# A fused attention block: the weighted sum moved between the two score passes, and the softmax denominator summed on GpSimd

## The chip, the core and the metric

The kernel runs on one core of one Trainium2 chip. The metric is device time in microseconds (us), the median of three runs. A profiled execution, recorded by the hardware profiler, has a time of its own.

The engines of the core are PE (TensorE, the matrix engine, with PEld for its weight loads), DVE (VectorE), ACT (ScalarE) and POOL (GpSimd); SP issues transfers. Each engine takes its instructions in the order in which the program has them, so an instruction that waits holds up everything behind it on that engine. Matmuls write to PSUM, a memory of eight banks per partition (a 128 x 512 float32 tile fills one).

## The reference

Layer norm with a modulation, causal attention with 32 query heads in 8 groups that share keys and values, a gated residual, then a second norm and a routed low-rank feed-forward part. The change is inside attention:

```python
q = _apply_rope((x @ Wq).reshape(b, t, 32, 32).transpose(0, 2, 1, 3), cos, sin)
k = _apply_rope((x @ Wk).reshape(b, t, 8, 32).transpose(0, 2, 1, 3), cos, sin)
v = (x @ Wv).reshape(b, t, 8, 32).transpose(0, 2, 1, 3)
...
scores = jnp.einsum('bhqd,bhkd->bhqk', q, k_h) / math.sqrt(HEAD_DIM)
scores = jnp.where(causal[None, None], jnp.finfo(scores.dtype).min, scores)
attn = jax.nn.softmax(scores, axis=-1)
ctx = jnp.einsum('bhqk,bhkd->bhqd', attn, v_h)
```

There are t = 2048 tokens, in float32; a head has 32 dimensions, and each of the 8 groups has 4 query heads, which together fill the 128 partitions.

## The kernel before

Three phases follow one another: norm and projections, attention, and the output projection with the feed-forward part. The attention phase lies between about 455 us and 2340 us of the profiled execution.

**Steps.** Attention is cut into 32 steps: for each group `g` of 8, four blocks `qb` = 0 to 3 of 512 queries. "Step 2" below is a step with `qb` = 2. A step looks at `nk = 4 * (qb + 1)` key tiles `kc` of 128 keys (4, 8, 12 and 16).

**Two score passes.** The softmax needs each query's maximum before it can exponentiate. The first pass (`maxima_units`, lines L344 to L378) computes scores with queries on the partitions: a unit is 4 matmuls (L358) for 128 queries and up to 512 keys, in two tiles `sm` of two banks each, which DVE reduces (L368; on the diagonal after adding the causal mask, L367). The second pass (`weights`, L407) computes them again with keys on the partitions: 4 matmuls (L414) into two tiles `sc`, to which small bfloat16 matmuls add the negated maxima (L422) and the causal mask (L431, on diagonal key tiles). ACT exponentiates each `sc` tile into `et` (L438).

**Sums.** `weighted_sum` (L444) multiplies `et` by the values into `po` (4 matmuls, L447). For odd `kc` POOL adds `et` of this key tile into `et` of the one before (L453), and `total` (L455) multiplies each such pair by a matrix of ones into `pd` (4 matmuls, L459): the denominators.

**Order.** While a step runs the second pass, it runs the first pass of the next step in between: step 0 has 8 units of the next step for its 4 key tiles, step 1 has 12 for 8, step 2 has 16 for 12, step 3 has 4 for 16. Per key tile the program has: units of the next step's maxima, `weights(kc)`, `weighted_sum(kc - 1)`, and on odd `kc` `total(kc - 3)` (`unit`, L464). At the end of a step `shift_rows` (L380) turns the next step's maxima into matmul rows: a cast, a subtraction, a cast, a subtraction and a cast on DVE (L384 to L388, on 128 x 16 elements), 4 transposes on PE (L391, tile `px`), and a copy `nt` (L395). `finish` (L472) then does the last sums, ACT copies `po` to `ctx` (L476), DVE takes the reciprocal `rd` of `pd` (L478) and POOL multiplies (L479). After each step 1, half of a modulation vector is computed (`mod_column_half` or `gate_half`, L121 to L146).

**Buffers.** `sm`, `sc`, `px` and the modulation tiles share one rotation of three two-bank PSUM tiles (`ps_s`, tag `sc`), so a tile is written only when the one three before it has been read. `po` and `pd` have a bank each. `et` has four buffers.

The scheduler of the language may move an instruction ahead of others on its engine; the order above is that of the program text.

Of the kernel before, what the change touches and what calls it, by code (L numbers as in the profile page):

```python
# [9 lines left out]
F32 = mybir.dt.float32  # L10
BF16 = mybir.dt.bfloat16
# [5 lines left out]
P = 128  # L17
# [3 lines left out]
HD = 32  # L21
# [3 lines left out]
QB = 512  # L25
# [9 lines left out]
def adaln_block_kernel(  # L35
# [16 lines left out]
    nc = tc.nc  # L52
# [68 lines left out]
    def mod_column_half(pool, pspool, tag, i, half):  # L121

        rows = mod_rows(pool, pspool, tag, i, half)
        pst = pspool.tile([P, 512], F32, tag=tag, name=f"modpt_{i}_{half}")
        for j in range(4):
            nc.tensor.matmul(
                pst[:, j : j + 1], rows[:, j * P : (j + 1) * P], ones_p[:, 0:1],
                start=True, stop=True,
            )
        dst = mod_cols[i][:, half * 4 : half * 4 + 4]  # L130
        if i in (1, 4):
            nc.vector.tensor_scalar_add(dst, pst[:, 0:4], 1.0)
        else:
            nc.vector.tensor_copy(dst, pst[:, 0:4])
# [34 lines left out]
    def modulate(dst, ps, scale, shift, k):  # L169
# [11 lines left out]
    q_t = [  # L181
        qpool.tile([P, T], F32, tag=f"q{g}", name=f"q{g}") for g in range(NG)
    ]

    with tc.tile_pool(name="kv", bufs=1) as kvpool:
# [4 lines left out]
        with tc.tile_pool(name="wqkv", bufs=1) as wp, tc.tile_pool(  # L190
            name="a_x", bufs=3
# [13 lines left out]
            with tc.tile_pool(name="m_w", bufs=4) as mp, tc.tile_pool(  # L205
                name="m_ps", bufs=2, space=PSUM
# [5 lines left out]
            with tc.tile_pool(name="a_h", bufs=2) as hp, tc.tile_pool(  # L212
                name="a_t", bufs=3
            ) as tp, tc.tile_pool(name="a_pt", bufs=2, space=PSUM) as ps_t, tc.tile_pool(
                name="a_pm", bufs=3, space=PSUM
# [76 lines left out]
        for i in (2, 5):  # L292
            gates[i] = gpool.tile([P, D], F32, tag=f"gate{i}", name=f"gate{i}")
        with tc.tile_pool(name="b_k", bufs=2) as kp, tc.tile_pool(
            name="b_e", bufs=4
        ) as ep, tc.tile_pool(name="b_s", bufs=2) as bp, tc.tile_pool(
            name="b_w", bufs=4
        ) as mp, tc.tile_pool(name="b_c", bufs=1) as bc, tc.tile_pool(
            name="b_ps", bufs=3, space=PSUM
# [80 lines left out]
            def shift_rows(n, g, qb, neg):  # L380

                nb = nbs[n % 2]
                rest = bp.tile([P, 4, 4], F32, tag="rest", name=f"rest_{g}_{qb}")
                nc.vector.tensor_copy(nb[:, :, :, 0], neg)  # L384
                nc.vector.tensor_sub(rest, neg, nb[:, :, :, 0])
                nc.vector.tensor_copy(nb[:, :, :, 1], rest)
                nc.vector.tensor_sub(rest, rest, nb[:, :, :, 1])
                nc.vector.tensor_copy(nb[:, :, :, 2], rest)  # L388
                px = ps_s.tile([P, 4, P], BF16, tag="sc", name=f"px_{g}_{qb}")
                for t in range(4):  # L390
                    nc.tensor.transpose(  # L391
                        px[:, t, :], nb[:, t].rearrange("p h r -> p (h r)"), ident_h
                    )
                nt = bp.tile([P, QB], BF16, tag="nt", name=f"nt_{g}_{qb}")
                nc.vector.tensor_copy(nt, px.rearrange("p t q -> p (t q)"))  # L395
                return nt

            def attend_units(g, qb, kr, nt):
                nk = 4 * (qb + 1)
                po = ps_o.tile([P, QB], F32, tag="po", name=f"po_{g}_{qb}")  # L400
                pd = ps_o.tile([P, QB], F32, tag="pd", name=f"pd_{g}_{qb}")
                ets = {}

                def offset(kc):
                    return max(0, kc * P - qb * QB)

                def weights(kc):  # L407

                    off = offset(kc)
                    ps = score_tiles(f"sc_{g}_{qb}_{kc}")  # L410
                    q0 = qb * QB
                    for j in range(4):
                        rows = slice(j * HD, (j + 1) * HD)
                        nc.tensor.matmul(  # L414
                            ps[j // 2][:, j % 2, off:],
                            kr[rows, kc * P : (kc + 1) * P],
                            q_t[g][rows, q0 + off : q0 + QB],
                            start=True, stop=False,
                        )
                    for j in range(4):  # L420
                        rows = slice(j * HD, (j + 1) * HD)
                        nc.tensor.matmul(  # L422
                            ps[j // 2][:, j % 2, off:], ones_h[rows, :], nt[rows, off:],
                            start=False, stop=(kc < 4 * qb),
                        )
                    if kc >= 4 * qb:
                        for c in range(4):
                            w = (c + 1) * HD
                            for j in range(4):
                                rows = slice(j * HD, (j + 1) * HD)  # L430
                                nc.tensor.matmul(  # L431
                                    ps[j // 2][:, j % 2, off : off + w],
                                    pick[rows, c, :], later[rows, c, :w],
                                    start=False, stop=(c == 3),
                                )
                    et = ep.tile([P, 4, QB], F32, tag="et", name=f"et_{g}_{qb}_{kc}")
                    for pr in range(2):
                        nc.scalar.activation(  # L438
                            et[:, 2 * pr : 2 * pr + 2, off:], ps[pr][:, :, off:],
                            AF.Exp, scale=1.0 / math.sqrt(HD),  # L440
                        )
                    ets[kc] = et

                def weighted_sum(kc):  # L444
                    off, et = offset(kc), ets[kc]
                    for j in range(4):
                        nc.tensor.matmul(  # L447
                            po[j * HD : (j + 1) * HD, off:], v_sb[:, kc, g, :], et[:, j, off:],
                            start=(kc == 0), stop=(kc == nk - 1),
                        )  # L450
                    if kc % 2 == 1:
                        a = ets[kc - 1]
                        nc.gpsimd.tensor_add(a[:, :, off:], a[:, :, off:], et[:, :, off:])  # L453

                def total(kc):  # L455

                    off, et = offset(kc), ets[kc]
                    for j in range(4):
                        nc.tensor.matmul(  # L459
                            pd[j * HD : (j + 1) * HD, off:], ones_k, et[:, j, off:],  # L460
                            start=(kc == 0), stop=(kc == nk - 2),
                        )

                def unit(kc):  # L464
                    if kc < nk:
                        weights(kc)
                    if 1 <= kc <= nk:
                        weighted_sum(kc - 1)
                    if kc >= 3 and kc % 2 == 1:
                        total(kc - 3)  # L470

                def finish():  # L472
                    unit(nk)
                    unit(nk + 1)
                    ctx_sb = bp.tile([P, QB], F32, tag="ctx", name=f"ctx_{g}_{qb}")
                    nc.scalar.copy(ctx_sb, po)  # L476
                    rd = bp.tile([P, QB], F32, tag="rd", name=f"rd_{g}_{qb}")
                    nc.vector.reciprocal(rd, pd)  # L478
                    nc.gpsimd.tensor_mul(  # L479
                        q_t[g][:, qb * QB : (qb + 1) * QB], ctx_sb, rd  # L480
                    )

                return [lambda kc=kc: unit(kc) for kc in range(nk)], finish


            rest = [(i, half) for i in (2, 3, 4, 5) for half in range(2)]
# [4 lines left out]
            for u in maxima_units(0, 0, 0, krs[0], state):  # L491
                u()
            nt = shift_rows(0, 0, 0, state["neg"])
            for n, (g, qb) in enumerate(steps):
                now, finish = attend_units(g, qb, krs[g], nt)
                ahead = []
                if n + 1 < len(steps):
                    g1, qb1 = steps[n + 1]
                    ahead = maxima_units(n + 1, g1, qb1, krs[g1], state)
                if qb == 1 and g + 1 < NG:  # L500
                    krs[g + 1] = keys(g + 1)
                done = 0
                for k, u in enumerate(now):
                    upto = len(ahead) * (k + 1) // len(now)
                    for a in ahead[done:upto]:
                        a()
                    done = upto
                    u()
                if n + 1 < len(steps):
                    nt = shift_rows(n + 1, g1, qb1, state["neg"])  # L510
                finish()
                if qb == 1:
                    i, half = rest[g]
                    if i in (3, 4):
                        mod_column_half(mp, ps_s, "sc", i, half)
                    else:
                        gate_half(mp, ps_s, "sc", i, half)


    with tc.tile_pool(name="c_w", bufs=1) as wp, tc.tile_pool(  # L520
# [146 lines left out]
```

## Time and profile before

| | us |
|---|---|
| runs | 2663.64, 2665.29, 2681.99 |
| median of the three | 2665.29 |
| the profiled execution | 2676.34 |
| its span, first to last instruction | 2674.6 |
| PE busy in the span | 2369.8 |
| DVE busy | 1267.6 |
| ACT busy | 631.5 |
| POOL busy | 634.8 |

One instance of each step, cut from one `ctx` copy (L476) to the next: step 2 from 1030.42 to 1112.23, step 3 to 1168.20, step 0 of the next group to 1207.97, step 1 to 1266.80.

How to read the profile: a group row gives line, engine, operation, tiles as output<-inputs, shapes and count, then busy time and the mean duration in ns of one, then idle time just before and what ended it. A timeline row gives start, duration, engine, line, operation, tiles, shapes and count of merged instructions, and in brackets the idle time before with its releaser. PEclk is the share of full speed granted to the TensorE clock. A float32 matmul appears as two matmul instructions, so 4 matmuls show as x8. Busy time of PE is modelled from starts, and pipelined matmuls overlap.

### The profile page before, as it was taken

To read this page: it belongs to the slowest core of one execution; us is meant where nothing else is said; L and a number is where in the kernel's file an instruction comes from. 1 tells how busy PE (TensorE), PEld (TensorE's weight loads), DVE (VectorE), ACT (ScalarE), POOL (GpSimd) and SP (SyncE) were. 2 spreads that over 40 slices of the span, in tenths; PEclk is the share of its full clock that TensorE was granted. 3 is DMA by queue.
4 is the path that set the end of the run, shared out by engine and by line. 5 is a ranking of instruction groups with operands and counts; after the bars stand their busy time and mean duration, and the time that the engine had idled before them with its cause. 6 is when DMAs were issued, how large, how long until landed. Compare 5 with 4: busy or idle time off the path is not lost.

```text
span 2674.6 us, 35449 instructions
## 1 busy us (share of the span) xinstructions
PE 2369.8 (89%) x15480; PEld 1081.7 (40%) x15480; DVE 1267.6 (47%) x2096; ACT 631.5 (24%) x869; POOL 634.8 (24%) x224
## 2 busy tenths in 40 slices
PE   6999997888888888888898888889888888889998
PEld 2888885323332333232333323223322322244544
DVE  3434324554554355446536544643654465243434
ACT  1001000224222422322241233224123322400101
POOL 0000001224323522432351243235123423500000
PEclk8999997789778978978896998889689788999999
DMA  7001002000000000000000000000000000021111
GB/s 277 27 24 36 12 5 63 0 33 1 16 32 1 17 1 32 1 17 5 28 14 4 32 1 17 9 24 11 7 32 1 1 1 1 23 105 47 48 63 48
DMA packets 29819, 74.73 MB, mean 28 GB/s; under 512 B 2784, under 2 KB 8032, under 8 KB 28640
## 3 DMA queue, kind: packets, MB, share of 16 engines
q1 hardware_dynamic: 25104, 65.03, 7.7%
q10 hardware_dynamic: 4560, 7.44, 0.8%
q8 instruction: 122, 2.00, 0.3%
q14 instruction: 33, 0.27, 0.0%
HBM read 55.68 MB, written 8.39 MB: 24 GB/s over the span
## 4 chain that ended last, share of the span: by engine, by line
PE 70%; DVE 21%; issue 4%; DMA 2%; ACT 2%; POOL 0%; SPq 0%; ACTq 0%; DVEq 0%; POOLq 0%
PE sc L414 14%; DVE mx L368 14%; PE po L447 11%; PE pq L271 10%; PE sm L358 10%; PE pw L546 8%; PE pd L459 5%; PE sc L422 3%; DVE rd L478 2%; PE pv L248 2%; ACT et L438 2%; PE sc L431 1%; PE pr L259 1%; DVE sm L367 1%; PE pa L570 1%
## 5 line engine op out<-in xcount | busy, mean ns | idle before, releaser
L368 DVE TENSOR_REDUCE mx<-sm 128x2 f32<-128x1024 f32 (+3 forms) x640 | 662.0, 1061 | 565.5 <-PE sm L358 558.6
L453 POOL TENSOR_TENSOR et<-et,et 128x2048 f32<-128x2048 f32 (+2 forms) x160 | 584.2, 3651 | 1088.4 <-ACT et L438 572.2
L438 ACT ACTIVATE et<-sc 128x1024 f32<-128x1024 f32 (+3 forms) x640 | 538.4, 893 | 1209.0 <-PE sc L431 614.5
L414 PE MATMUL sc<-q,kr 32*128 32x512 f32 (+3 forms) x2560 | 587.5, 648 | 137.8 <-DVE mx L368 129.4
L358 PE MATMUL sm<-kr,q 32*128 32x512 f32 (+3 forms) x2560 | 475.7, 665 | 73.3 <-DVE mx L368 66.7
L414 PEld LDWEIGHTS sc<-q,kr 32*128 32x128 f32 x2560 | 200.6, 205 | 489.1 <-DVE mx L368 208.2
L447 PE MATMUL po<-et,v_sb 128*32 128x512 f32 (+3 forms) x2560 | 368.5, 617 | 0.0
L358 PEld LDWEIGHTS sm<-kr,q 32*128 32x128 f32 x2560 | 177.6, 214 | 392.8 <-issue 159.5
L546 PE MATMUL pw<-wo,q 128*128 128x512 f32 x512 | 226.1, 599 | 12.1 <-DVE wo L533 12.1
L367 DVE TENSOR_TENSOR sm<-sm,causal 128x256 f32<-128x256 f32 x256 | 105.6, 424 | 272.1 <-PE sm L358 272.0
L271 PE MATMUL pq<-h_t,wq 128*128 128x256 f32 x1024 | 231.5, 379 | 0.0
L422 PE MATMUL sc<-nt,ones_h 32*128 32x512 bf16 (+3 forms) x1280 | 225.6, 390 | 0.0
L271 PEld LDWEIGHTS pq<-h_t,wq 128*128 128x128 f32 x1024 | 194.6, 190 | 26.5
L459 PE MATMUL pd<-et,ones_k 128*32 128x512 f32 (+1 forms) x1280 | 191.7, 677 | 1.1 <-POOL et L453 1.1
L546 PEld LDWEIGHTS pw<-wo,q 128*128 128x128 f32 x512 | 96.6, 192 | 129.8 <-issue 118.4
L478 DVE RECIPROCAL rd<-pd 128x512 f32<-128x512 f32 x32 | 107.4, 3358 | 62.3 <-PE pd L459 62.3
L275 DVE TENSOR_TENSOR u<-pq,cs 128x256 f32<-128x256 f32 x80 | 33.9, 424 | 215.2 <-PE pq L271 215.1
L447 PEld LDWEIGHTS po<-et,v_sb 128*32 128x32 f32 x2560 | 55.8, 115 | 142.7 <-issue 132.1
L431 PE MATMUL sc<-later,pick 32*128 32x64 bf16 (+3 forms) x2048 | 108.9, 212 | 0.0
L304 POOL MEMSET ones_h<- 128x128 bf16 x1 | 0.2, 204 | 433.1 <-DVE q L260 433.1
L550 DVE TENSOR_TENSOR cx<-pw,cx 128x512 f32<-128x512 f32 x32 | 22.1, 692 | 166.8 <-PE pw L546 162.7
L172 ACT ACTIVATE h_t<-pt,mod,mod 128x128 f32<-128x128 f32 x64 | 27.8, 457 | 260.1 <-PE pt L229 258.4
(101 smaller groups left out, 1273.4 us busy)
## 6 DMA issues: line engine op xcount, KB each, us to landing
wmod<-in_wmod_dram SPq DMA_DIRECT2D x48, 512.0 KB, 5.7
xt<-in_x_dram SPq DMA_DIRECT2D x16, 512.0 KB, 4.3
kr<-k SPq DMA_DIRECT2D x32, 256.0 KB, 4.4
cx<-in_x_dram SPq DMA_DIRECT2D x16, 512.0 KB, 4.4
out_dram<-ot SPq DMA_DIRECT2D x16, 512.0 KB, 2.9
wq<-in_wq_dram ACTq DMA_DIRECT2D x8, 512.0 KB, 9.8
wo<-in_wo_dram SPq DMA_DIRECT2D x8, 512.0 KB, 7.2
wv_sb<-in_wv_dram ACTq DMA_DIRECT2D x1, 1024.0 KB, 10.1
```

The lines of the kernel that those rows point to most:

```text
L271: nc.tensor.matmul(ps, w, h_t[:, k, :], start=(k == 0), stop=(k == NC - 1))
L358: nc.tensor.matmul(ps[j // 2][:, j % 2, :nk], q_t[g][rows, q0 : q0 + P], kr[rows, kc * QB : kc * QB + nk], start=True, stop=True,)
L368: nc.vector.tensor_reduce(mx[:, 2 * pr : 2 * pr + 2, kc], ps[pr][:, :, :nk], AX.X, ALU.max)
L414: nc.tensor.matmul(ps[j // 2][:, j % 2, off:], kr[rows, kc * P : (kc + 1) * P], q_t[g][rows, q0 + off : q0 + QB], start=True, stop=False,)
L422: nc.tensor.matmul(ps[j // 2][:, j % 2, off:], ones_h[rows, :], nt[rows, off:], start=False, stop=(kc < 4 * qb),)
L431: nc.tensor.matmul(ps[j // 2][:, j % 2, off : off + w], pick[rows, c, :], later[rows, c, :w], start=False, stop=(c == 3),)
L438: nc.scalar.activation(et[:, 2 * pr : 2 * pr + 2, off:], ps[pr][:, :, off:], AF.Exp, scale=1.0 / math.sqrt(HD),)
L447: nc.tensor.matmul(po[j * HD : (j + 1) * HD, off:], v_sb[:, kc, g, :], et[:, j, off:], start=(kc == 0), stop=(kc == nk - 1),)
L453: nc.gpsimd.tensor_add(a[:, :, off:], a[:, :, off:], et[:, :, off:])
L459: nc.tensor.matmul(pd[j * HD : (j + 1) * HD, off:], ones_k, et[:, j, off:], start=(kc == 0), stop=(kc == nk - 2),)
L478: nc.vector.reciprocal(rd, pd)
L546: nc.tensor.matmul(ps, q_t[k][:, t * P : (t + 1) * P], wo_sb[k][:, cols], start=(k == 0), stop=(k == NC - 1),)
```

## The change

The denominators are no longer summed by PE over pairs. Key tile 0 writes its exponentials into a tile of its own (`sum`, two buffers), POOL adds those of every other key tile into it, and one denominator matmul per head is made per step. `et` has three buffers in place of four. Per key tile, the weighted sum of the tile before now comes ahead of `weights(kc)`, after the maxima units. The denominator, the reciprocal and the multiplication (`divide`) are put off to key tile 2 of the next step, and the multiplication is on DVE. `px`, the denominator and the modulation tiles now share one bank (`ps_o`, tag `px`) in place of the rotation's tiles. The modulation halves move to key tile 3 of step 2.

```diff
-            name="b_e", bufs=4
+            name="b_e", bufs=3
...
-                px = ps_s.tile([P, 4, P], BF16, tag="sc", name=f"px_{g}_{qb}")
+                px = ps_o.tile([P, 4, P], BF16, tag="px", name=f"px_{g}_{qb}")
...
-                    et = ep.tile([P, 4, QB], F32, tag="et", name=f"et_{g}_{qb}_{kc}")
+                    if kc == 0:
+                        et = ep.tile([P, 4, QB], F32, tag="sum", name=f"sum_{g}_{qb}", bufs=2)
+                    else:
+                        et = ep.tile([P, 4, QB], F32, tag="et", name=f"et_{g}_{qb}_{kc}")
...
-                    if kc % 2 == 1:
-                        a = ets[kc - 1]
+                    if kc > 0:
+                        a = ets[0]
                         nc.gpsimd.tensor_add(a[:, :, off:], a[:, :, off:], et[:, :, off:])
 
-                def total(kc):
-
-                    off, et = offset(kc), ets[kc]
+                def last():
+
+                    weighted_sum(nk - 1)
+                    ctx_sb = bp.tile([P, QB], F32, tag="ctx", name=f"ctx_{g}_{qb}")
+                    nc.scalar.copy(ctx_sb, po)
+                    return ctx_sb
+
+                def divide(ctx_sb):
+
+                    pd = ps_o.tile([P, QB], F32, tag="px", name=f"pd_{g}_{qb}")
                     for j in range(4):
                         nc.tensor.matmul(
-                            pd[j * HD : (j + 1) * HD, off:], ones_k, et[:, j, off:],
-                            start=(kc == 0), stop=(kc == nk - 2),
+                            pd[j * HD : (j + 1) * HD, :], ones_k, ets[0][:, j, :],
+                            start=True, stop=True,
                         )
...
                     nc.vector.reciprocal(rd, pd)
-                    nc.gpsimd.tensor_mul(
-                        q_t[g][:, qb * QB : (qb + 1) * QB], ctx_sb, rd
-                    )
+                    nc.vector.tensor_mul(q_t[g][:, qb * QB : (qb + 1) * QB], ctx_sb, rd)
...
-                for k, u in enumerate(now):
-                    upto = len(ahead) * (k + 1) // len(now)
+                for kc in range(nk):
+                    upto = len(ahead) * (kc + 1) // nk
                     for a in ahead[done:upto]:
                         a()
                     done = upto
-                    u()
+                    if kc > 0:
+                        weighted_sum(kc - 1)
+                    weights(kc)
+                    if kc == 2 and behind is not None:
+                        behind()
+                        behind = None
+                    if kc == 3 and qb == 2:
+                        i, half = rest[g]
+                        if i in (3, 4):
+                            mod_column_half(mp, ps_o, "px", i, half)
+                        else:
+                            gate_half(mp, ps_o, "px", i, half)
                 if n + 1 < len(steps):
                     nt = shift_rows(n + 1, g1, qb1, state["neg"])
-                finish()
-                if qb == 1:
-                    i, half = rest[g]
-                    if i in (3, 4):
-                        mod_column_half(mp, ps_s, "sc", i, half)
-                    else:
-                        gate_half(mp, ps_s, "sc", i, half)
+                ctx_sb = last()
+                behind = lambda divide=divide, ctx_sb=ctx_sb: divide(ctx_sb)
+            behind()
```

In the instruction order that the scheduler makes of the changed program, the first of the four denominator matmuls of a step 3 stands earlier than in the text: behind the first two maxima units of the next step 0 and ahead of that step's first score matmul (in seven of the eight groups; the last step has no next one). In a step 3, for key tiles without a maxima unit, the first score matmul of `kc` stands ahead of `weighted_sum(kc - 1)` and the other three behind it. On DVE, one reduction or mask addition of key tile 3 stands between the reciprocal and the multiplication of `divide`, the others behind.

More of the change, by code (lines that the diff above doesn't have):

```diff
@@ L400, in attend_units @@
                 po = ps_o.tile([P, QB], F32, tag="po", name=f"po_{g}_{qb}")
-                pd = ps_o.tile([P, QB], F32, tag="pd", name=f"pd_{g}_{qb}")
                 ets = {}
@@ L450, in weighted_sum @@
                         )
-                    if kc % 2 == 1:
-                        a = ets[kc - 1]
+                    if kc > 0:
+                        a = ets[0]
                         nc.gpsimd.tensor_add(a[:, :, off:], a[:, :, off:], et[:, :, off:])
-                def total(kc):
-                    off, et = offset(kc), ets[kc]
+                def last():
[5 more added lines that the diff above has]
+                    pd = ps_o.tile([P, QB], F32, tag="px", name=f"pd_{g}_{qb}")
                     for j in range(4):
                         nc.tensor.matmul(
-                            pd[j * HD : (j + 1) * HD, off:], ones_k, et[:, j, off:],
-                            start=(kc == 0), stop=(kc == nk - 2),
-                        )
[L464 to L476, printed above, removed]
+                            pd[j * HD : (j + 1) * HD, :], ones_k, ets[0][:, j, :],
+                            start=True, stop=True,
+                        )
                     rd = bp.tile([P, QB], F32, tag="rd", name=f"rd_{g}_{qb}")
                     nc.vector.reciprocal(rd, pd)
-                    nc.gpsimd.tensor_mul(
-                        q_t[g][:, qb * QB : (qb + 1) * QB], ctx_sb, rd
-                    )
-                return [lambda kc=kc: unit(kc) for kc in range(nk)], finish
+                    nc.vector.tensor_mul(q_t[g][:, qb * QB : (qb + 1) * QB], ctx_sb, rd)
+                return nk, weights, weighted_sum, last, divide
             rest = [(i, half) for i in (2, 3, 4, 5) for half in range(2)]
@@ L493, in adaln_block_kernel @@
             nt = shift_rows(0, 0, 0, state["neg"])
+            behind = None
             for n, (g, qb) in enumerate(steps):
-                now, finish = attend_units(g, qb, krs[g], nt)
+                nk, weights, weighted_sum, last, divide = attend_units(g, qb, krs[g], nt)
                 ahead = []
@@ L507, in adaln_block_kernel @@
                     done = upto
-                    u()
+                    if kc > 0:
[3 more added lines that the diff above has]
+                        behind()
+                        behind = None
+                    if kc == 3 and qb == 2:
[4 more added lines that the diff above has]
+                            gate_half(mp, ps_o, "px", i, half)
                 if n + 1 < len(steps):
                     nt = shift_rows(n + 1, g1, qb1, state["neg"])
-                finish()
-                if qb == 1:
-                    i, half = rest[g]
-                    if i in (3, 4):
-                        mod_column_half(mp, ps_s, "sc", i, half)
-                    else:
-                        gate_half(mp, ps_s, "sc", i, half)
+                ctx_sb = last()
+                behind = lambda divide=divide, ctx_sb=ctx_sb: divide(ctx_sb)
+            behind()
     with tc.tile_pool(name="c_w", bufs=1) as wp, tc.tile_pool(
```

## The prediction

> **What bounds the kernel now.** I read the page's busy row, clock row and chain first:
>
> ```profile
> PE 2369.8 (89%) x15480; PEld 1081.7 (40%) x15480; DVE 1267.6 (47%) x2096; ACT 631.5 (24%) x869; POOL 634.8 (24%) x224
> ...
> PEclk8999997789778978978896998889689788999999
> ...
> PE 70%; DVE 21%; issue 4%; DMA 2%; ACT 2%; POOL 0%; SPq 0%; ACTq 0%; DVEq 0%; POOLq 0%
> PE sc L414 14%; DVE mx L368 14%; PE po L447 11%; PE pq L271 10%; PE sm L358 10%; PE pw L546 8%; PE pd L459 5%; PE sc L422 3%; DVE rd L478 2%; PE pv L248 2%; ACT et L438 2%; PE sc L431 1%; PE pr L259 1%; DVE sm L367 1%; PE pa L570 1%
> ```
>
> PE bounds the whole, DVE's maxima take turns with it, POOL is nowhere on the chain. The denominators (L459) hold 5% of the span, the reciprocal 2%. But shares are means, so next the groups with shapes kept apart, and the four steps one by one (step 2, 3, 0, 1; columns: length, busy PE, PEld, DVE, ACT, POOL, clock, DMA):
>
> ```profile
> L368 DVE TENSOR_REDUCE mx<-sm 128x2 f32<-128x1024 f32 x448 | 532.4, 1220 | 561.1 <-PE sm L358 558.6
> L453 POOL TENSOR_TENSOR et<-et,et 128x2048 f32<-128x2048 f32 x96 | 433.7, 4518 | 531.7 <-ACT et L438 360.0 <-PE po L447 140.0 <-PE sm L358 31.7
> L453 POOL TENSOR_TENSOR et<-et,et 128x1536 f32<-128x1536 f32 x32 | 109.6, 3425 | 297.6 <-PE po L447 187.8 <-ACT et L438 109.8
> L453 POOL TENSOR_TENSOR et<-et,et 128x512 f32<-128x512 f32 x32 | 40.9, 1279 | 259.1 <-PE po L447 156.8 <-ACT et L438 102.4
> L478 DVE RECIPROCAL rd<-pd 128x512 f32<-128x512 f32 x32 | 107.4, 3358 | 62.3 <-PE pd L459 62.3
> ```
>
> ```profile
> 1030.06:1112.23 82.17, 71.72 (x520) 24.64 (x516) 44.73 (x54) 21.29 (x26) 23.97 (x7) 0.87 0.08 27
> 1112.23:1168.20 55.97, 51.28 (x492) 17.30 (x484) 15.78 (x27) 29.05 (x33) 33.13 (x9) 0.97 0.06 13
> 1168.20:1207.97 39.77, 33.61 (x236) 14.51 (x228) 24.85 (x36) 5.78 (x10) 5.99 (x3) 0.61 0.05 11
> 1207.97:1268.00 60.03, 51.55 (x376) 17.92 (x372) 35.03 (x45) 14.12 (x18) 15.02 (x5) 0.83 0.00 1
> ```
>
> A full POOL add takes 4.52 us. Step 3 takes 56 us for 16 key tiles, 3.5 each, with half of the adds that the change wants, and POOL is busy there for 33 already. That is the stage to look at. The timeline of one key tile with one maxima unit, in step 2, shows the order's part:
>
> ```profile
> 1079.29 1.18 PE L358 MATMUL sm<-kr,q 32*128 32x512 f32 x8
> 1080.26 1.13 PE L414 MATMUL sc<-q,kr 32*128 32x512 f32 x4
> 1080.46 2.36 DVE L368 TENSOR_REDUCE mx<-sm 128x2 f32<-128x1024 f32 x2 [2.37 <-PE sm L358]
> 1081.74 0.70 PE L414 MATMUL sc<-q,kr 32*128 32x512 f32 x2 [0.36 <-DVE mx L368]
> 1082.93 1.94 ACT L438 ACTIVATE et<-sc 128x1024 f32<-128x1024 f32 x2 [2.73 <-PE sc L422]
> 1083.01 1.06 PE L447 MATMUL po<-et,v_sb 128*32 128x512 f32 x8
> ```
>
> The second half of the scores waits until the first `sm` tile is reduced; the key tile takes 4.72 us without `pd` (1079.29 to 1084.01). Last, DVE's small operations beside POOL's adds:
>
> ```profile
> 1204.80 0.20 DVE L384 CAST nb<-neg 128x16 bf16<-128x16 f32 x1
> ...
> 1205.50 1.31 POOL L453 TENSOR_TENSOR et<-et,et 128x512 f32<-128x512 f32 x1 [13.96 <-PE po L447]
> 1205.71 1.16 DVE L388 CAST nb<-rest 128x16 bf16<-128x16 f32 x1
> ```
>
> A cast takes 0.20 alone and 1.16 when an add has begun: it ends just after the add. The subtractions (L385, L387), two inputs in SBUF, go from 0.18 to 1.14 to 1.23 in the same way. Reductions and the reciprocal, which read PSUM, never change.
>
> **Steps 1 and 2, main part.** All per group, in the profile's time. E is the end of a key tile's score matmuls; the exponentials are done at E + 1.13 and E + 2.10 (timeline, 1127.44 to 1129.54). With the weighted sum behind a maxima unit, the first half of the unit runs at once, the second needs the tile that the first exponential frees and ends at about E + 2.0; weighted sum 1.0 from E + 2.1, scores 1.28, next E at + 4.4, the reduction by now hidden. So 4.72 becomes 4.4. With two units (1065.05 to 1072.2, 7.1) the same walk, DVE's reductions 1.15 apart, gives 6.2. Step 1 has four of each: 4 x 0.3 + 4 x 0.9 = 4.9 saved; step 2 eight and four: 6.2. Denominators at 0.86 to 1.75 each, 0.95 taken: 3.5 saved in step 1 (4), 4.8 in step 2, 1.7 in step 0 (two, at its clock 0.61, less the new one). POOL, 4.52 per tile, hides behind 5.0 on average there.
>
> **The divide moved to key tile 2.** At the step's start it is gone: reductions started at 1211.74 behind the reciprocal and could at 1208.9: 2.3 saved in steps 1 and 2, counting only what `pd` did not. In its new place: `pd` E to E + 1.0 (mostly beside the exponentials, 0.4 net), reciprocal to E + 4.5, and queued behind it on DVE the reductions of key tile 3, for which PE's scores wait. First reduction done at E + 5.65. The multiplication has no row; by the subtractions it waits for an add running since E + 2.1, until 6.65, and takes 0.7 (DVE's 128x512 additions, L550, 692 ns); bounds 0 and 4.5. Next E is + 7.0 in step 2 for 4.8: 2.2 lost. In step 1, two units: + 11.4 for 6.6: 4.8 lost. In step 0, POOL idle by then: 2.7 lost.
>
> **The modulation halves.** Column halves cost the same 4 us as now. Gate halves (four of eight) bring two DVE operations within SBUF beside nearly unbroken adds, which they run without now (0.43 and 0.68). Bounds 0 and 4.5 each; nearest rows are the held casts and subtractions; 3.6 for both, as POOL itself starves meanwhile: 1.5 per group.
> One rule to weigh: the Trainium skill, "SBUF — State Buffer", section "Who interferes with whom", lets a VectorE `tensor_scalar` take the port pair shared with GpSimd only in a two-port mode, and then wait for a whole GpSimd instruction. No row shows L144 (`tensor_scalar`) beside an add: without that mode the 3.6 would be near 0, 1.8 less per group; with it, it stands.
>
> **Step 3.** Time 0 is the `ctx` copy (1112.23). E of key tile 0 is 3.2; the first weighted sum now waits for the exponentials before three of four score matmuls go: E1 = 7.5, first add from 9.6. E2 = 11.8, then the divide: reciprocal to 16.3, multiplication behind the second add (14.1 to 18.6) to 19.3, so the scores of key tile 3 end at about 20.9 and its exponentials at 23.0, where POOL has idled for 4.4. Ten adds of 4.52 (key tiles 3 to 12), with hand-over 4.54, end at 68.4; then 3.43, 2.35 (no row at 1024; between 3.43 and 1.28) and 1.28: 75.5. PE and ACT alone, period 4.3 (2.1 exponentials, 0.9 half a weighted sum, 1.3 scores), end their last scores at 72.3. Each of the five shift-row operations then meets an add that has begun, so they end with the last one at 76.3; transposes and last weighted sum to 77.2. Now 55.97: **21.2 lost**. Where POOL slips among them it costs 3 less.
>
> **Step 0.** The early denominator matmul waits for the last add, 75.5, which is earlier than the shift rows; it holds nothing. First scores come 4.2 after `ctx` rather than 6.1 (1168.20 to 1174.32): 1.9 saved. Order at half clock, PE full: 1.0 saved.
>
> **Sum per group.** Step 0: - 1.9 - 1.7 - 1.0 + 2.7 = - 1.9. Step 1: - 4.9 - 3.5 - 2.3 + 4.8 + 0.4 = - 5.5. Step 2: - 6.2 - 4.8 - 2.3 + 2.2 + 0.4 + 1.5 = - 9.2. Step 3: + 21.2. Together + 4.6, times 8 = 37. The last step 3 has no step 0 behind it (+ 2), no maxima unit that could starve POOL at key tile 3, and ends with adds, `pd`, reciprocal and product bare: 9.6 + 12 x 4.54 + 7.06 + 1.0 + 3.4 + 0.7 = 76.2 for 51.3 now (2290.06 to 2341.34), 4 more than the 21.2. So + 43 on 2676.3 = 2719. That execution lies 11 above the median 2665.3, so I forecast **2708**. SP's transfers and the two fewer `et` tiles cost nothing: `kr` and `wmod` land steps ahead, and `et` is held by POOL's chain, counted above.
>
> **The rivals.**
> *Clock up in steps 1 and 2 (faster).* The clock there is 0.83 and 0.87, 0.97 in step 3. With fewer waits it could reach 0.97: 60 x (1 - 0.83/0.97) = 8.7 and 82 x (1 - 0.87/0.97) = 8.5 per group, - 137 in all: 2570. It turns the sign from 5.4 per group on, about a clock higher by 0.03 in both. Against it: the 2 to 5 us holes at key tile 3 take the place of those at the starts. Chance 0.2.
> *The locks hide.* If the shift rows get through between adds (- 3), the multiplication and gate operations never wait (- 5 in step 3 and its starved POOL, - 1.5), step 3 costs 13: - 9.5 per group, 2632; half of it 2670. Within 1% for the larger part. Chance 0.22.
> *Clock down in step 3.* Its PE would be busy for 3.97 of each 4.54 us (gaps of 0.2, 0.1 and 0.27 where it waits for ACT). Between 1105 and 1115 PE was busy for 78% of the time, without a gap above 1.3 us, and the clock was 0.67. At half clock a key tile takes 6.4 instead of 4.54; for half of 12 tiles, 11 per group: 2797. Against it: between 1095 and 1105 PE was busy for 86% and kept the full clock. Chance 0.18.
> The Trainium skill, "TensorE: Matmul & The Clock Gate", section "What's actually happening", asks for an idle window of about 3.4 us before the clock halves; by it this rival costs 0, while the row above shows a fall without one.
>
> **How the numbers follow.** The forecast has 0.4, within 2670 to 2750. One per cent, 26.7 us, is about what a measurement tells from no change. Faster by more: the first rival, and the low end of the second and of an overestimated step 3: 0.2. Within: most of the second and the lower part of the forecast: 0.24. Slower: 0.56. The range cuts half of the first rival and the far end of the last: 2625 to 2790.
>
> **What would show it.** POOL busy near 36 x 8 = 288 adds: per group 24 x 4.52 + 4 x (3.43 + 2.35 + 1.28) = 137, in all 1094 us. Step 3 near 77 us with POOL busy for 90% of its middle and `et` released by POOL; casts and subtractions of 1 to 4 us at its end; a hole of 2 to 5 us in PE at key tile 3 of every step; steps 1 and 2 at 54 and 73. Step 3 below 68, or a clock above 0.9 in steps 1 and 2, would make the forecast wrong on the fast side; a clock below 0.85 in step 3 on the slow side.

## The result, and the profile after

The changed kernel takes 2747.0 us (median of 4 runs, 2744.9 to 2753.2) against 2664.5: a ratio of 1.0305, 95% interval 1.025 to 1.036. It is slower. The profiled execution has a span of 2743.2. From its page, the busy row and the clock row:

```profile
PE 2437.8 (89%) x14456; PEld 1071.1 (39%) x14456; DVE 1340.8 (49%) x2128; ACT 632.4 (23%) x869; POOL 1101.9 (40%) x320
...
PEclk8999997789888888888988888788788888999999
```

PE has 1024 matmuls less and is busy for 68 us more (its busy time is modelled: the eight matmuls of a weighted sum count 1.97 us in the timeline below, and 1.06 us in the prediction's). POOL's busy time has gone from 635 to 1102. The chain of this page follows the work back through the last tenth of the span only, so the steps have to be read one by one. The same four steps, in the order 2, 3, 0, 1 (length, busy PE, PEld, DVE, ACT, POOL, clock, DMA):

```profile
1031.99:1106.91 74.92, 70.07 (x472) 23.22 (x473) 46.74 (x54) 21.30 (x26) 43.19 (x11) 0.86 0.09 29
1106.91:1190.13 83.22, 66.44 (x432) 19.65 (x431) 20.52 (x28) 29.15 (x33) 61.25 (x15) 0.87 0.06 13
1190.13:1224.51 34.38, 30.18 (x217) 11.81 (x217) 24.88 (x35) 5.78 (x9) 7.04 (x3) 0.75 0.00 1
1224.51:1277.65 53.14, 47.56 (x340) 16.82 (x340) 36.45 (x45) 13.53 (x17) 25.11 (x7) 0.85 0.00 1
```

Steps 0, 1 and 2 are 5 to 7 us shorter than before, step 3 is 27 longer. The timeline of step 3, with the exponentials (L441) and weighted sums (L450) of key tiles 7 and 8, shows a step that alternates between ACT and PE, and POOL at work all the time:

```profile
1144.09 43.99 POOL L456 TENSOR_TENSOR sum<-sum,et 128x2048 f32<-128x2048 f32 x11
...
1150.65 1.94 ACT L441 ACTIVATE et<-sc 128x1024 f32<-128x1024 f32 x2 [2.48 <-PE sc L421]
1151.72 1.97 PE L450 MATMUL po<-et,v_sb 128*32 128x512 f32 x8 [0.33 <-ACT et L441]
1153.62 0.70 PE L413 MATMUL sc<-q,kr 32*128 32x512 f32 x3
1153.87 1.02 PE L413 MATMUL sc<-q,kr 32*128 32x512 f32 x5
1155.06 1.94 ACT L441 ACTIVATE et<-sc 128x1024 f32<-128x1024 f32 x2 [2.47 <-PE sc L421]
1156.13 1.97 PE L450 MATMUL po<-et,v_sb 128*32 128x512 f32 x8 [1.16 <-ACT et L441]
```

From one weighted sum (L450) to the next it is 4.41 us. ACT waits 2.5 us for the scores, which stand behind the weighted sum, which waits for ACT; the weighted sum itself takes 1.97 instead of 1.06, because its second half has to wait for the second exponential. POOL needs 4.52 per key tile. These are two chains of nearly the same length, and these rows do not say which of them makes the step long.

At key tile 3 of the same step there is a hole, by `divide`:

```profile
1120.21 3.36 DVE L474 RECIPROCAL rd<-pd 128x512 f32<-128x512 f32 x1 [13.50 <-PE pd L469]
1123.49 0.41 DVE L367 TENSOR_TENSOR sm<-sm,causal 128x256 f32<-128x256 f32 x1
1123.80 2.70 DVE L475 TENSOR_TENSOR q<-ctx,rd 128x512 f32<-128x512 f32 x1
1126.43 0.41 DVE L368 TENSOR_REDUCE mx<-sm 128x2 f32<-128x256 f32 x1
1126.99 1.77 PE L413 MATMUL sc<-q,kr 32*128 32x512 f32 x4 [3.44 <-DVE mx L368]
...
1130.39 4.50 POOL L456 TENSOR_TENSOR sum<-sum,et 128x2048 f32<-128x2048 f32 x1 [4.43 <-ACT et L441]
...
1139.50 9.12 POOL L456 TENSOR_TENSOR sum<-sum,et 128x2048 f32<-128x2048 f32 x2 [4.61 <-ACT et L441]
```

The multiplication takes 2.70 us, 0.68 of work and the rest waiting; it ends at 1126.50, 0.55 us after the second of the two POOL adds that the trace shows back to back from 1116.84 for 9.11 us (to 1125.95). The reduction behind it is late, PE waits 3.44 us, and POOL runs dry twice, for 4.4 and 4.6 us. The second time PE was slow. The granted clock (the last column but two) between the reduction and 1140.00, and then to 1180.00, was

```profile
1126.43:1140.00 13.57, 11.85 (x36) 2.62 (x36) 1.33 (x5) 2.96 (x3) 5.00 (x2) 0.62 0.00 0
1140.00:1180.00 40.00, 33.60 (x250) 10.35 (x248) 5.35 (x10) 17.02 (x18) 39.37 (x9) 1.00 0.00 1
```

0.62 at first, and full after it. In each of the seven steps 3 that have a next step, POOL runs dry this second time for 4.6 us. At the end of the step the first two of the five shift-row operations meet an add:

```profile
1184.86 1.93 DVE L384 CAST nb<-neg 128x16 bf16<-128x16 f32 x1
1186.83 1.29 DVE L385 TENSOR_TENSOR rest<-neg,nb 128x16 f32<-128x16 f32 x1
```

They take 3.2 us where 0.4 would do, and PE waits 2.61 us for them.

### The profile page after: what moved, and what is told of

It reads as the page before. It is cut to its first block, busy times and chain, and to the rows that moved or that the text cites. A ratio compares the mean times of both kernels' runs of the same rounds, so it can differ in the third digit from the quotient of the medians.

```text
span 2743.2 us, 33738 instructions
## 1 busy us (share of the span) xinstructions
PE 2437.8 (89%) x14456; PEld 1071.1 (39%) x14456; DVE 1340.8 (49%) x2128; ACT 632.4 (23%) x869; POOL 1101.9 (40%) x320
## 5 line engine op out<-in xcount | busy, mean ns | idle before, releaser
L456 POOL TENSOR_TENSOR sum<-sum,et 128x2048 f32<-128x2048 f32 (+3 forms) x288 | 1092.8, 3795 | 877.6 <-ACT et L441 866.3
L368 DVE TENSOR_REDUCE mx<-sm 128x2 f32<-128x1024 f32 (+3 forms) x640 | 669.6, 1061 | 357.2 <-PE sm L358 349.8
L358 PE MATMUL sm<-kr,q 32*128 32x512 f32 (+3 forms) x2560 | 656.2, 648 | 98.0 <-DVE mx L368 59.8
L441 ACT ACTIVATE et<-sc 128x1024 f32<-128x1024 f32 (+3 forms) x576 | 477.2, 879 | 1115.4 <-PE sc L421 674.2
L450 PE MATMUL po<-et,v_sb 128*32 128x512 f32 (+3 forms) x2304 | 396.3, 589 | 68.2 <-ACT et L441 68.2
L358 PEld LDWEIGHTS sm<-kr,q 32*128 32x128 f32 x2560 | 225.1, 207 | 403.6 <-ACT et L441 165.1
L450 PEld LDWEIGHTS po<-et,v_sb 128*32 128x32 f32 x2304 | 64.2, 114 | 338.2 <-ACT et L441 186.7
L441 ACT ACTIVATE sum<-sc 128x1024 f32<-128x1024 f32 x64 | 62.0, 1021 | 150.2 <-PE sc L421 93.9
L430 PE MATMUL sc<-later,pick 32*128 32x32 bf16 (+3 forms) x2048 | 86.7, 202 | 0.0
```

The lines of the kernel that those rows point to most:

```text
L358: nc.tensor.matmul(ps[j // 2][:, j % 2, :nk], q_t[g][rows, q0 : q0 + P], kr[rows, kc * QB : kc * QB + nk], start=True, stop=True,)
L368: nc.vector.tensor_reduce(mx[:, 2 * pr : 2 * pr + 2, kc], ps[pr][:, :, :nk], AX.X, ALU.max)
L430: nc.tensor.matmul(ps[j // 2][:, j % 2, off : off + w], pick[rows, c, :], later[rows, c, :w], start=False, stop=(c == 3),)
L441: nc.scalar.activation(et[:, 2 * pr : 2 * pr + 2, off:], ps[pr][:, :, off:], AF.Exp, scale=1.0 / math.sqrt(HD),)
L450: nc.tensor.matmul(po[j * HD : (j + 1) * HD, off:], v_sb[:, kc, g, :], et[:, j, off:], start=(kc == 0), stop=(kc == nk - 1),)
```

## Experiments

The theory at this point: each of two chains, PE waiting for ACT by the new order and POOL's adds, is enough by itself to make step 3 long. Its rivals: it is POOL alone, or the order alone. Four runs undo one or both, or the multiplication on DVE.

**The order undone.**

```diff
-                    if kc > 0:
-                        weighted_sum(kc - 1)
                     weights(kc)
+                    if kc > 0:
+                        weighted_sum(kc - 1)
```

> The changed kernel with one thing undone: weights(kc) again ahead of weighted_sum(kc - 1). Two chains of about the same length run in step 3 of the changed kernel: POOL's adds, 4.52 us each, and PE waiting for ACT, 4.41 us per key tile. Theory 'either chain is enough': undoing the order leaves POOL's chain, step 3 goes from 83 to about 73, and steps 1 and 2 lose what the order saved, 4.9 and 6.2; time 2735 to 2765 (changed kernel 2747). Rival 'the order alone': step 3 falls to about 60, time 2650. Rival 'POOL alone': step 3 stays at 83, time 2835.

Measured: 2767.3 us, ratio to the kernel before 1.036 (1.033 to 1.040), just above what the theory gave. Step 3 fell from 83.1 to 68.2, not to 60, where the theory had about 73; step 2 rose to 81.2 as expected, step 1 did not (53.2), and step 0 rose from 34.4 to 45.0, which was not expected. Neither rival holds in its pure form. Part of step 3's fall only moved into step 0: the transposes of the shifted rows, which stood 1.3 us ahead of the `ctx` copy, now start 4.8 to 6.1 behind it, as the shift-row operations wait for the last adds, and the first exponentials of step 0 end 5.4 later. And POOL now holds ACT, by the `et` tiles that its adds still read:

```profile
ACT et L441 <- POOL sum L456: 155.9, 60, 4.8
```

(waiter, awaited, total us, times, longest). The changed kernel's list of waits has no such wait.

**Half of the adds.** The other half of the key tiles is left out of the denominators.

```diff
-                    if kc > 0:
+                    if kc % 2 == 1:
                         a = ets[0]
```

> The changed kernel with POOL adding odd key tiles only, which leaves half of the weights out of the denominators; four small bfloat16 matmuls per step add 128 to each denominator, so that none is zero. Theory 'either chain is enough': PE and ACT keep step 3 at 4.41 per key tile; it goes from 83 to 77 to 80 by shorter locks at its end and behind the divide, other steps by about 1 each; time 2690 to 2725. Rival 'POOL alone': step 3 falls to about 60, time 2560. Rival 'the order alone': no change, 2740.

Measured: 2695.5, ratio 1.0085 (1.006 to 1.011). The time is within what the theory gave; step 3 is 74.4, for 77 to 80. POOL alone is out, and so is the order alone, by which there would be no change.

**Both undone**, with the same half left out of the denominators.

> Scores first again and half of the adds (the other half is left out of the denominators, and 128 added as in the run before). Theory 'either chain is enough': only now step 3 falls, to about 60; steps 1 and 2 are 5 and 6 longer than in the changed kernel; time 2630 to 2665. Both rivals: the same as the run that undoes their own cause, 2650 for the order, 2650 for POOL less what the order saves in steps 1 and 2, so this run tells them apart only beside the other two.

Measured: 2675.7, ratio 1.0015 (0.999 to 1.004). Step 3 is 56.0, as in the kernel before (55.5), for about 60. So the theory held in kind, while the time is 11 us above its range: step 0 is 45.0. It also says something unpleasant: with both costs out of step 3, the rest of the change (16 of a group's 20 denominator passes gone, the divide put off, `px` in its own bank, the product on DVE) gains nothing in the sum. Step 1 is 5.1 us shorter than before the change, step 2 0.9, and step 0 is 6.3 longer.

**The product on POOL again.**

```diff
-                    nc.vector.tensor_mul(q_t[g][:, qb * QB : (qb + 1) * QB], ctx_sb, rd)
+                    nc.gpsimd.tensor_mul(q_t[g][:, qb * QB : (qb + 1) * QB], ctx_sb, rd)
```

> The changed kernel with the multiplication of divide on POOL again, so that DVE's reductions of key tile 3 stand behind the reciprocal only. Theory: the multiplication held DVE for 2.7 us in step 3 (0.7 of work, 2.0 of waiting for an add) and PE with it for 3.4, after which the clock fell to half; step 3 gets 4 to 8 shorter, steps 1 and 2 by 1 to 2 each; time 2670 to 2715. Rival 'the reciprocal itself, 3.36 us on DVE, makes the hole': within 15 us of the changed kernel, 2735 to 2750. If POOL is so full that 32 products of 1.26 us each delay its adds, step 3 gets 1.3 longer instead, 2755.

Measured: 2701.4, ratio 1.0106 (1.008 to 1.0135), within what the theory gave. Step 3 is 76.8, its clock 0.92 for 0.87; step 1 is 1.0 shorter, step 2, for which 1 to 2 were expected, is not. So 2747.0 - 2701.4 = 46 us of the loss are one operation of 0.68 us on the wrong engine, 32 times.

The next four take the kernel before or the changed one and do some part of the change alone.

**The order alone, in steps 0 to 2**, in the kernel before:

```diff
                 def unit(kc):
+                    if qb < 3 and 1 <= kc <= nk:
+                        weighted_sum(kc - 1)
                     if kc < nk:
                         weights(kc)
-                    if 1 <= kc <= nk:
+                    if qb == 3 and 1 <= kc <= nk:
                         weighted_sum(kc - 1)
```

> The kernel before with one thing done: the weighted sum ahead of the scores in steps 0, 1 and 2, old order in step 3; denominators, divide and tiles as before. The first four runs give the order's effect as the difference of the two runs with half of the adds: step 0 from 45.0 to 33.8, step 1 from 54.9 to 55.3, step 2 from 81.1 to 75.4, step 3 from 56.0 to 74.4. Theory 'the order earns where a maxima unit stands between, and costs in step 3': 5 to 11 less in step 0, 0 to 5 in step 1, 6 in step 2, nothing in step 3; ratio to the kernel before 0.95 to 0.97. Rival 'the saving of steps 0 to 2 came from the denominators and the divide': 0.99 to 1.01.

Measured: 2531.9, ratio 0.949 (0.943 to 0.955), at the edge of what the theory gave. By steps it was less exact: 3.4 us less in step 0, 8.5 in step 1, 8.1 in step 2, 0.4 more in step 3. It is the fastest kernel of the study that computes everything, together with the one after the next. Its busy row and the same four steps:

```profile
PE 2276.8 (90%) x15480; PEld 1060.5 (42%) x15480; DVE 1274.0 (51%) x2096; ACT 631.7 (25%) x869; POOL 634.3 (25%) x224
```

```profile
978.41:1053.27 74.86, 68.75 (x512) 23.25 (x508) 45.14 (x53) 21.29 (x26) 24.03 (x7) 0.89 0.09 29
1053.27:1109.49 56.22, 52.97 (x492) 17.70 (x484) 15.95 (x27) 29.05 (x34) 33.16 (x9) 0.93 0.06 13
1109.49:1145.13 35.64, 28.38 (x232) 12.63 (x228) 25.04 (x36) 5.78 (x9) 5.96 (x3) 0.73 0.06 12
1145.13:1196.53 51.40, 46.14 (x364) 16.69 (x360) 34.52 (x43) 13.54 (x18) 14.99 (x5) 0.86 0.00 1
```

All engines do the same work as before, with the same instruction counts, in 133 us less. The wait that the order was to cover (waiter, awaited, total us, times, longest) went, from the kernel before to this run, from the first line to the second:

```profile
PE sc L414 <- DVE mx L368: 129.4, 193, 2.7
PE sc L414 <- DVE mx L368: 45.6, 63, 1.7
```

That is 84 of the 133 us. The granted clock of steps 0 to 2 is higher too (0.73, 0.86 and 0.89 in the rows above, for 0.61, 0.83 and 0.87 before); how much of the gain is the clock's was not separated.

**The order alone, in all steps:** the same with the condition on `qb` dropped.

> The kernel before with the weighted sum ahead of the scores in all steps, POOL with its half of the adds as before. Theory: step 3 from 55.5 to between 70 and 75, by the wait for ACT that no maxima unit covers, the other steps as in the run with steps 0 to 2 alone: 8 x 15 to 19 us, 120 to 155, longer than that run; ratio to before 1.00 to 1.03. Rival 'step 3 was POOL's': the same as that run, 0.95 to 0.97.

Measured: 2670.3, ratio 1.0006 (0.998 to 1.003). Step 3 is 75.5, a little over what the theory gave: the order gives in three steps what it takes back in the fourth. POOL's timeline in its step 3 has

```profile
1114.88 4.52 POOL L453 TENSOR_TENSOR et<-et,et 128x2048 f32<-128x2048 f32 x1 [4.24 <-ACT et L438]
1123.65 4.52 POOL L453 TENSOR_TENSOR et<-et,et 128x2048 f32<-128x2048 f32 x1 [4.25 <-ACT et L438]
1132.42 4.51 POOL L453 TENSOR_TENSOR et<-et,et 128x2048 f32<-128x2048 f32 x1 [4.25 <-ACT et L438]
```

one add every 8.77 us, for two key tiles: 4.39 per key tile, with POOL idle half of the time. Here POOL cannot be the cause.

**The late divide**, added to the order in steps 0 to 2: the reciprocal and the product (on POOL) at key tile 2 of the next step.

```diff
+                    if k == 2 and behind is not None:
+                        behind()
+                        behind = None
```

> The kernel of the run with the new order in steps 0 to 2, and the reciprocal and product (on POOL) put off to key tile 2 of the next step. By the prediction's terms the late divide saves 2.3 at the start of steps 1 and 2 and loses 2 to 3 at key tile 3 of steps 0, 1 and 2: within 1.5% of that run, rather slower. Rival 'the start of a step was the better part of the gain': 2% or more faster than it.

Measured: 2528.4, ratio 0.946 (0.939 to 0.952), the same as without it (0.949). But the divide did not move. In this run's trace, too, every reciprocal stands behind the `ctx` copy of its own step, 0.4 to 0.9 us after the copy begins, and every product about 4 us after it, as in the run without the edit:

```profile
1145.04 0.59 ACT L478 COPY ctx<-po 128x512 f32<-128x512 f32 x1 [3.29 <-PE po L447]
1145.96 3.36 DVE L483 RECIPROCAL rd<-pd 128x512 f32<-128x512 f32 x1 [1.11 <-PE pd L459]
```

The order of the program text is not the order on the engine here, so this run measures the order alone a second time, and neither the theory nor its rival. What a late divide does can be read where it did move: in the changed kernel with the product on POOL, beside the run with the order alone in all steps. In step 1 the exponentials of key tile 0 end 6.6 us behind the `ctx` copy rather than 8.9, so 2.3 sooner; key tile 3 then takes 10.7 us rather than 5.9. In steps 0 and 2 key tile 3 takes 3.5 and 2.5 longer. (A key tile's time is from the end of the exponentials before to the end of its own, in the ACT timeline, as a mean over the groups.)

**The changed kernel with both mends**: product on POOL, old order in step 3.

> The changed kernel with the product on POOL and the old order in step 3 only. Theory: steps 0 to 2 stay at 34, 53 and 75, step 3 is POOL's chain alone, 65 to 68 (68.2 in the first run, less the hole behind the divide), against 55.5 in the kernel before; 228 to 230 per group for 236: ratio to before 0.97 to 0.985. Rival 'the two chains only hide one another': step 3 stays near 77 and the ratio at 1.01.

Measured: 2651.3, ratio 0.994 (0.991 to 0.997); expected were 0.97 to 0.985. Step 3 is 64.9 as foreseen, but step 0 is 39.7 and not 34. In its step 3 POOL's chain is the one that holds:

```profile
1083.20 9.12 POOL L456 TENSOR_TENSOR sum<-sum,et 128x2048 f32<-128x2048 f32 x2 [10.30 <-PE po L450]
1092.29 1.26 POOL L475 TENSOR_TENSOR q<-ctx,rd 128x512 f32<-128x512 f32 x1
1093.51 49.42 POOL L456 TENSOR_TENSOR sum<-sum,et 128x2048 f32<-128x2048 f32 x11
```

From 1083.20 to 1142.93 POOL does not rest once, in a step cut from 1075.18 to 1140.88, and ACT waits for it (`et` L441 for `sum` L456) for 168.1 us in 65 waits. What step 0 has gained in length, 5.3 us over the run with the product alone on POOL, lies ahead of its first exponentials. There two shift-row subtractions of 0.18 us wait for the last adds, partly behind the `ctx` copy:

```profile
1139.54 3.44 DVE L385 TENSOR_TENSOR rest<-neg,nb 128x16 f32<-128x16 f32 x1
...
1143.25 2.18 DVE L387 TENSOR_TENSOR rest<-rest,nb 128x16 f32<-128x16 f32 x1
```

So steps 3 and 0 have to be read together: 104.6 us here, and 87.3 with half of the adds (the last run below).

Two last runs ask what taking the denominators off PE is worth at all.

**One denominator pass per step**, in the kernel with the order in steps 0 to 2. All pairs but the first are left out of the denominators.

```diff
-                    if kc >= 3 and kc % 2 == 1:
+                    if kc == 3:
                         total(kc - 3)
```

> The kernel with the order alone in steps 0 to 2 (2532), with one denominator pass per step in place of nk/2: only the first pair of key tiles is summed on PE, the other pairs are left out of the denominators, and 128 is added to each so that none is zero; POOL adds pairs as before. It shows what the denominator matmuls cost PE once the order is mended. Theory 'they are PE work on the path': 16 passes per group less, 0.86 each at full clock, 14 per group, 110 in all: 2410 to 2450. Rival 'they fill PE's waits': within 25 of that run, 2505 to 2555.

Measured: 2482.0, ratio 0.930 (0.927 to 0.932): 50 us for 128 passes, 0.39 each, less than half of their 0.86. Step 3 is 49.2 for 55.9. Steps 0, 1 and 2 are 35.0, 52.7 and 74.9, against 35.3, 51.5 and 73.9 with all passes; their clock went from 0.73, 0.85 and 0.92 to 0.74, 0.80 and 0.86. Neither the theory nor its rival met this size.

It does not follow that the passes cost nothing in steps 0 to 2, because this edit does a second thing. `pd` is complete after key tile 3, and the reciprocal now runs there, ahead of reductions that PE waits for (a step 2):

```profile
999.72 3.36 DVE L487 RECIPROCAL rd<-pd 128x512 f32<-128x512 f32 x1 [2.33 <-PE pd L466]
...
1004.21 1.12 PE L416 MATMUL sc<-q,kr 32*128 32x512 f32 x2 [1.48 <-DVE mx L370]
```

Key tile by key tile, against the run with all passes: the exponentials of key tile 0 end 1.5 us sooner in steps 1 and 2; key tiles 4 and 5, behind the reciprocal, take 2.5 and 1.8 longer in step 1, and 3.0 and 1.3 in step 2; those behind a pass that is gone (6 in step 1; 6, 8 and 10 in step 2) take 0.6, and 0.2, 1.0 and 0.6 less. In step 3 key tiles 6, 8, 10, 12 and 14 each take 0.9 to 1.0 less. The last two passes of a step stand behind its last scores, and leaving them out made the ends of steps 1 and 2 no shorter. So a pass between two key tiles cost PE 0.2 to 1.0 us, and in steps 1 and 2 the reciprocal hid the gain.

**The changed kernel with its mends and half of the adds** (the other half left out of the denominators).

> The changed kernel with the product on POOL, the old order in step 3, and half of the adds (the others left out of the denominators, 128 added to each): one denominator pass per step, late divide, tiles as in the change, POOL's chain no longer the length of step 3. Theory: step 3 at 53 to 56, steps 0 to 2 at 34 to 40, 52 and 75 as in the run with all adds: 217 to 224 per group, 2520 to 2590, so the change without its two costs in step 3 is no faster than the order alone. Rival 'the denominators off PE are worth their price': 2410 to 2470.

Measured: 2511.4, ratio 0.939 (0.935 to 0.943), 9 us below what the theory gave: step 3 is 50.6 and not 53 to 56. That is 1% below the order alone, with adds left out that the result needs, and 29 us above the run with one denominator pass, which makes as many adds: beside it, the rest of the change (the late divide, the tiles, the place of the modulation halves) costs more than it gives.

The step lengths, from one `ctx` copy to the next, as means over the groups (us; the last step 3, which has no next step, is apart):

| kernel | step 0 | step 1 | step 2 | step 3 | last step 3 |
|---|---|---|---|---|---|
| before | 38.7 | 60.0 | 82.0 | 55.5 | 44.8 |
| the change | 34.4 | 53.9 | 75.1 | 83.1 | 66.7 |
| order undone | 45.0 | 53.2 | 81.2 | 68.2 | 67.4 |
| half the adds | 33.8 | 55.3 | 75.4 | 74.4 | 66.7 |
| both undone | 45.0 | 54.9 | 81.1 | 56.0 | 45.3 |
| product on POOL | 34.4 | 52.9 | 75.4 | 76.8 | 67.0 |
| order alone, 0 to 2 | 35.3 | 51.5 | 73.9 | 55.9 | 46.4 |
| order alone, all | 34.2 | 50.7 | 74.6 | 75.5 | 68.0 |
| the divide late in the text only | 35.6 | 51.7 | 74.4 | 56.3 | 44.8 |
| the change, both mends | 39.7 | 52.2 | 75.7 | 64.9 | 64.3 |
| one denominator pass | 35.0 | 52.7 | 74.9 | 49.2 | 40.2 |
| both mends, half the adds | 36.7 | 52.6 | 75.6 | 50.6 | 44.0 |

The last column is the cleanest answer. Without maxima units and their holes, the step is 66.7 to 68.0 by the order alone, 64.3 to 67.4 by the adds alone, 66.7 with both, and 40 to 46 with neither: a maximum of two chains, not a sum. In the other seven steps 3 of the changed kernel the order is the chain that sets the pace: from key tile 6 on, each key tile takes the same time as in the run with the order alone in all steps, within 0.1 us, where POOL idles half of the time. The adds come on top by what waits for them: 75.5 by the order alone and 6.3 by the product on DVE make 81.8 of the 83.1, and the shift rows wait at the step's end.

## Why the prediction was right, and where its terms were not

**The total.** Forecast 2708, + 43; measured 2747, + 82.5. Sign and range were right, the size about half. Per group the forecast had + 4.6; the traces give - 4.3 - 6.1 - 6.9 + 27.6 = + 10.3, against - 1.9 - 5.5 - 9.2 + 21.2.

**POOL's work** was right: 1092.8 us for 288 adds, with 1094 forecast; the shape that had no row took 2344 ns, with 2.35 taken.

**Step 3** had the right parts. First add: forecast at 9.6 us, measured at 9.9 (1116.84 - 1106.91). The add behind the divide: 23.0, measured 23.5. The end went differently. The forecast has ten adds without a rest behind the divide, and POOL's chain ending last. In the trace POOL adds once, runs dry again for 4.6 us, and only then works without a rest to the last add, which ends at 81.2 (1188.08) where the forecast had 75.5. Two things were behind this. The clock was put at no cost in the forecast and into a rival: behind the wait of 3.44 us it was 0.62 over 13.6 us, and key tile 4 took 9.1 us instead of 4.4 (means of the groups, here and with the order alone in all steps). Where the prediction puts this rival at 0 for want of a long idle window, it left out its own hole at key tile 3, forecast at 2 to 5 us and measured at 3.44. With the hole taken away by the product on POOL, step 3 lost 6.3 us and took 76.8, near the 77.2 of the forecast. The rival "clock down in step 3" thus came true for 14 us of each step, not for half of it. And "PE and ACT alone, period 4.3" was taken for the shorter chain; its period is 4.41, of which PE waits 1.16 for ACT where 0.27 was taken, and it set the pace from key tile 6 on. With the product on POOL it still does, so that the 76.8 there meets the 77.2 is in part luck.

**The other rivals.** The clock of steps 1 and 2 did not rise clearly (0.85 and 0.86 in the four steps shown, for 0.83 and 0.87). The locks did not hide, as follows.

**The locks.** That the multiplication would wait for an add was right: 1709 ns on the mean of 32, 680 when free. Of the five shift-row operations at the end of a step 3 only two met an add, where the forecast had five, but the second of the two ends with the last add (1188.12 and 1188.08), so that the step ends soon behind that add, as forecast (2.0 us, for 1.7); in the step shown the two take 2.8 us more than alone. Of the gate operations, L144 waited in three of four times (2.07 us at the median, 0.43 free): 1.6 rather than 3.6 for both. L146 took 0.68 each time, but no add was running beside it, so its lock was not put to the test. The Trainium skill, "SBUF — State Buffer", section "Who interferes with whom", had L144 among the operations that can take the shared port pair, and the run agrees.

**Steps 0 to 2** came out near the forecast (- 4.3, - 6.1 and - 6.9 for - 1.9, - 5.5 and - 9.2), but that their sums agree (- 17.3 for - 16.6) is luck: two terms were wrong in opposite ways. The order is worth more than its terms: alone in all steps it gives 4.5, 9.3 and 7.4 us, where 1.0, 4.9 and 6.2 were counted. The term that failed is "Denominators at 0.86 to 1.75 each, 0.95 taken: 3.5 saved in step 1, 4.8 in step 2, 1.7 in step 0". It multiplies a price by all passes. Against the run with the order alone in all steps, the key tiles of the changed kernel behind a pass that is gone are 0.6 us shorter in step 1 (key tile 6) and 0.2, 1.0 and 0.6 in step 2 (6, 8 and 10), the same as in the run with one denominator pass. So about 0.6 and 1.8 us were saved, and no gain shows for the passes behind a step's last scores. The denominators' share of 5% of the chain of waits was read as time to be had; the part that lies at the end of a step was not.

**The late divide** was forecast to lose a little more than it gains, and it did where it moved: 2.3 us saved at the start of step 1 with the product on POOL, as forecast, and at key tile 3 3.5, 4.8 and 2.5 lost in steps 0, 1 and 2, for 2.7, 4.8 and 2.2. With the product on DVE key tile 3 lost 4.0, 6.0 and 2.4. Put together, the changed kernel is 0.2, 3.2, 0.5 and 7.6 us longer in steps 0 to 3 than the order alone in all steps, which by itself is as fast as the kernel before: all of the loss is in what came with the order, 46 of the 82.5 us by the product on DVE.

**The early denominator matmul** held nothing, as forecast: it began at 1194.11, the last add had ended at 1188.08.

What stays open is the clock. No run shows what lowered it in steps 1 and 2 of the run with one denominator pass (0.80 and 0.86 for 0.85 and 0.92), and none measures the order in steps 0 to 2 with the denominators on POOL and the divide at the step's start.

## What to carry to other kernels

Moving a matmul so that it covers one engine's latency uncovers another's: the weighted sum hides DVE's reduction where a maxima unit stands next to it, and exposes ACT's exponentials where none does, so the order has to follow what stands between, step by step. Before work goes to a slow engine, hold its time per tile against the period of the stage that has the least time, not against its share of the span: 24% over all was 59% in step 3. And an operation of 0.7 us that has to wait for that engine costs what it waits for and everything queued behind it. Last, look in the trace whether an edit of the program's order reached the engine: here one did not, and its run looked like a measured zero.

## What the runs showed of the hardware

After one wait of 3.44 us PE's granted clock was 0.62 over 13.6 us, though PE was busy for 11.85 of them; it was full again while PE still waited 1.16 us of every 4.41. A GpSimd add of two 128 x 2048 float32 tiles took 4.52 us at the mean, within 0.01, in every run; DVE is the one that waited, a subtraction of 0.18 us for up to 3.44.
